# A graph layer with a routed feed-forward: compares and half of the scaling move from VectorE to GpSimd

## The chip, the cores and the metric

One core of a Trainium2 chip runs the kernel as one program. The metric is the device time of one execution in microseconds (us); the shorter the better. The engines are TensorE (PE, with its weight loads as PEld), VectorE (DVE), ScalarE (ACT), GpSimd (POOL) and SyncE (SP, here only an issuer of DMAs).

## The reference, cut to what matters

There are 6250 nodes with 256 features, 100,000 edges sorted by destination, and 4 heads of 64 features.

```python
h = layernorm(x)
messages = (h @ Wf.T)[src] * direction[:, 0:1] + (h @ Wr.T)[src] * direction[:, 1:2]
scores = leaky_relu(einsum('ef,hf->eh', messages, attn[0]), 0.2)
e = exp(scores - scores.max(axis=0))
norm = e / (segment_sum(e, dst)[dst] + 1e-10)
x = x + concat over heads of segment_sum(messages * norm[:, head], dst)
# then: a top-1 router over 8 experts with a capacity, relu feed-forward 256 -> 1024 -> 256 in the
# chosen expert, times the router's probability, added to x
```

What the change touches is the message of an edge: the row of the source node has a forward half and a reverse half, each is scaled by a number of that edge, and they are added. Then every message goes to its destination's sum.

## The kernel before, in words

**Node table.** A first stage normalises the nodes, multiplies them with both weight matrices and writes a table `node_tab` to memory, one row of 136 numbers per node: 68 forward (64 features and 4 score parts) and 68 reverse.

**Tiles and batches.** The edges lie in 782 tiles of 128, one edge per partition. `order` lists 66 batches of tiles: 64 of them have GB = 12 tiles, one has 4 and the last has 10. GT = 6 is half a batch. `srci` holds the source node of each edge, `ea` its two factors, `local` the place of its destination among the at most 128 nodes of its group.

**One batch** goes through these functions:

- `gathers(b)` (L983): for each tile one indirect DMA on GpSimd's queue (L989) that fetches 128 rows of the table into one of three `gt` buffers. In the second half of a batch it also issues waiting `put` calls (L1198): scatters of routed rows into the experts' buffer `buf`, one behind a gather.
- `messages(b)` (L995): on VectorE, copies both factors of the batch into `fixed`, which lies in PSUM (L1002), scales the forward halves in place (L1004, 128x816), then for each half batch scales the reverse halves into the PSUM tile `rv` (L1009) and adds both into `m` (L1011); then the scores (L1014 to L1022) and on ScalarE their exponentials (L1024).
- `places(b)` (L1027): one VectorE compare (L1032, 128x1536) that makes `hot`, for each tile a 128x128 matrix of zeros and ones which says to which destination each edge belongs. Its operands are the column numbers (`lane_p`, in `fixed`) and `local`.
- `products(b)` (L1035): VectorE spreads message times weight over the four heads (L1041, 128x3072).
- `windows(b, half)` (L1054): TensorE adds up the messages by destination, one matmul per tile with `hot` as weights (L1073); finished groups are copied and stored to `sums`.

**The order of work** is written out by hand (the pools run under a manual schedule). The loop over b from 0 to NB = 66 calls `messages(b)`, `windows(b - 1, 0)`, `places(b)`, `products(b)`, `windows(b - 1, 1)`, and, at its end, `gathers(b + 3)`; three batches of gathers are issued ahead of the loop. Between these calls stand pieces of two other jobs: the router for nodes whose sums are complete (`route`, which among much else runs L1121 and L1122 on VectorE and hands the `put` calls to the gathers), and, from b = 13, pieces of the experts' feed-forward (L1351 and L1369 on TensorE). How many pieces go between two calls is fixed by written-down costs when the program is built. Behind the loop come the rest of the router and the rest of the feed-forward, and the fetching of results (L1401). Each engine works through its own queue in this order.

Of the kernel before, what the change touches and what calls it, by code (L numbers as in the profile page):

```python
# [8 lines left out]
F32 = mybir.dt.float32  # L9
I32 = mybir.dt.int32  # L10
AF = mybir.ActivationFunctionType
OP = mybir.AluOpType
AX = mybir.AxisListType

P = 128
# [504 lines left out]
def kernel(  # L520
# [27 lines left out]
    nc = tc.nc  # L548
# [13 lines left out]
    MS = O + H  # L562
    ROW = 2 * MS
# [6 lines left out]
    GB = 12  # L570
# [10 lines left out]
    GT = GB // 2  # L581
# [24 lines left out]
    node_tab = dram.tile([N, ROW], F32, name="node_tab")  # L606
# [38 lines left out]
    lane = const.tile([P, P], F32, name="lane")  # L645
# [55 lines left out]
    srci = ep.tile([P, EW], I32, name="srci")  # L701
    ea = ep.tile([P, 2, EW], F32, name="ea")
    local = ep.tile([P, ET], F32, name="local")
# [45 lines left out]
    with tc.tile_pool(name="p1", bufs=2) as p1, \  # L749
# [19 lines left out]
        for c, tiles in enumerate(parts):  # L769
            k = len(tiles)  # L770
# [86 lines left out]
    def clear(r):  # L857

        nc.sync.dma_start(buf[r:r + 512, 0:D].rearrange("(p n) d -> p n d", n=4),
                          zeros.rearrange("p (n d) -> p n d", n=4))  # L860

    def clear_last(e):

        r0, r1 = e * TOT + OFF[NP - 2], (e + 1) * TOT
        J = (r1 - r0) // P
        nc.sync.dma_start(ybuf[r0:r1, :].rearrange("(p n) d -> p (n d)", n=J), zeros[:, 0:J * D])
        r0 = e * TOT + OFF[NP - 1]
        J = (r1 - r0) // P
        nc.sync.dma_start(buf[r0:r1, D:BW].rearrange("(p n) k -> p n k", n=J),
                          zeros[:, 0:J * (D + 2)].rearrange("p (n k) -> p n k", k=D + 2))  # L870
# [7 lines left out]
    order = [(i, min(i + GB, TOP)) for i in range(HEAD, TOP, GB)]  # L878
# [3 lines left out]
    NB = len(order)  # L882
# [59 lines left out]
    with tc.tile_pool(name="p4", bufs=1) as p4, tc.tile_pool(name="p5", bufs=2) as p5, \  # L942
# [3 lines left out]
        p2 = edge_pools.enter_context(tc.tile_pool(name="p2", bufs=2))  # L946
# [4 lines left out]
        lane_p, shift_p = fixed[:, 0:P], fixed[:, P:P + H]  # L951

        def turn(b, k0, k1):
            o = P + H + b % 2 * (2 + H) * GB
            return fixed[:, o + k0 * GB:o + k1 * GB]

        def spread(t):

            pm = ps2.tile([P, H, P], F32, name="pm", tag="acc", bufs=4)
            for hd in range(H):  # L960
                nc.tensor.transpose(pm[:, hd, :], t[:, hd:hd + 1].to_broadcast([P, P]), ident)
            return pm
# [16 lines left out]
            got.append(over)  # L979


        gts, vs = {}, {}
        pool_work = []  # L983

        def gathers(b):
            i0, i1 = order[b]
            gts[b] = p2.tile([P, GB, ROW], F32, name="gt", bufs=3)
            for i in range(i0, i1):
                nc.gpsimd.indirect_dma_start(  # L989
                    out=gts[b][:, i - i0, :], out_offset=None, in_=node_tab,  # L990
                    in_offset=bass.IndirectOffsetOnAxis(ap=srci[:, i:i + 1], axis=0))
                if i - i0 >= GT and pool_work:
                    pool_work.pop(0)()

        def messages(b):  # L995

            i0, i1 = order[b]
            n = i1 - i0
            gt = gts.pop(b)
            m = p2.tile([P, GB, MS], F32, name="m")  # L1000
            fac = turn(b, 0, 2).rearrange("p (k j) -> p k j", k=2)
            nc.vector.tensor_copy(fac[:, :, :n], ea[:, :, i0:i1])  # L1002
            fw = gt[:, :n, 0:MS]
            nc.vector.tensor_mul(fw, fw, fac[:, 0, :n].unsqueeze(2).to_broadcast([P, n, MS]))  # L1004
            for a0 in range(0, n, GT):
                a1 = min(a0 + GT, n)
                k = a1 - a0
                rv = ps2.tile([P, GT, MS], F32, name="rv")
                nc.vector.tensor_mul(rv[:, :k, :], gt[:, a0:a1, MS:ROW],  # L1009
                                     fac[:, 1, a0:a1].unsqueeze(2).to_broadcast([P, k, MS]))  # L1010
                nc.vector.tensor_add(m[:, a0:a1, :], fw[:, a0:a1, :], rv[:, :k, :])  # L1011
            sc = p2.tile([P, GB, H], F32, name="sc")
            s = sc[:, :n, :]
            nc.vector.scalar_tensor_tensor(s, m[:, :n, O:MS], 0.2, m[:, :n, O:MS],  # L1014
                                           op0=OP.mult, op1=OP.max)
            if i1 == ET:
                nc.vector.tensor_scalar(sc[:, n - 1, :], sc[:, n - 1, :], no_edge, None, op0=OP.add)
            nc.vector.tensor_reduce(gmax[:, b, :], s.rearrange("p j h -> p h j"), AX.X, OP.max)
            if b == 0:
                nc.vector.tensor_reduce(shift, spread(gmax[:, 0, :]), AX.X, OP.max)  # L1020
                nc.vector.tensor_copy(shift_p, shift)
            nc.vector.tensor_sub(s, s, shift_p.unsqueeze(1).to_broadcast([P, n, H]))  # L1022
            v = p2.tile([P, GB, ACC], F32, name="v")
            nc.scalar.activation(v[:, :n, H * O:ACC], s, AF.Exp)  # L1024
            vs[b] = m, v

        def places(b):  # L1027

            i0, i1 = order[b]
            n = i1 - i0  # L1030
            hot = p2.tile([P, GB, P], F32, name="hot")
            nc.vector.tensor_tensor(hot[:, :n, :], lane_p.unsqueeze(1).to_broadcast([P, n, P]),  # L1032
                                    local[:, i0:i1].unsqueeze(2).to_broadcast([P, n, P]), OP.is_equal)
            vs[b] += (hot,)

        def products(b):
            n = order[b][1] - order[b][0]
            m, v, hot = vs[b]
            w = turn(b, 2, 2 + H).rearrange("p (j h) -> p j h", h=H)
            nc.vector.tensor_copy(w[:, :n, :], v[:, :n, H * O:ACC])  # L1040
            nc.vector.tensor_mul(  # L1041
                v[:, :n, 0:H * O].rearrange("p n (h o) -> p n h o", h=H),
                m[:, :n, 0:O].unsqueeze(2).to_broadcast([P, n, H, O]),
                w[:, :n, :].unsqueeze(3).to_broadcast([P, n, H, O]))

            vl = p2.tile([P, ACC], F32, name="vl")
            nc.scalar.copy(vl, v[:, n - 1, :])  # L1047
            vs[b] = v, hot, vl

        taken = {"released": 0, "passes": 0, "before": None, "pv": None, "rows": 0, "jobs": 0, "fetched": 0}  # L1050

# [376 lines left out]
        def routes_of(c):  # L1428
            nonlocal next_p
            for cost in route(c, next_p):  # L1430
                yield cost
            if chunks[c][-1] == LASTS[next_p]:
                end_pass(next_p)
                wait_pass.append(next_p)
                next_p += 1
                if next_p < NP:
                    begin_pass(next_p)
                yield 0.0

        def step_routing():  # L1440
            nonlocal credit
            while routing:
                cost = next(routing[0], None)
                if cost is None:
                    routing.pop(0)
                    continue
                credit -= cost
                break

        def step_experts(share):  # L1450
            nonlocal credit
            credit = min(credit + share, share)
            while credit > 0 and b > 12:
                cost = step_ffn()
                if cost is None:
                    break
                credit -= cost

        for b in range(3):
            gathers(b)  # L1460
        for b in range(NB + 1):
            if 4 <= b < 4 + E:
                clear(1024 * (b - 4))
                clear(1024 * (b - 4) + 512)
                clear_last(b - 4)
            if b < NB:
                messages(b)
            step_routing()
            if b:
                windows(b - 1, 0)  # L1470
            step_experts(SHARE / 2)
            step_routing()
            if b < NB:
                places(b)
            step_routing()
            if b < NB:
                products(b)
            step_routing()
            if b:
                windows(b - 1, 1)  # L1480
            taken["released"] = taken["rows"]
            step_experts(SHARE / 2)
            while next_c < len(chunks) and done_at[next_c] < b:
                routing.append(routes_of(next_c))
                next_c += 1
            step_routing()
            pool_work.extend(todo)
            del todo[:]
            if b + 3 < NB:
                gathers(b + 3)  # L1490
            if wait_pass and not pool_work:
                taken["rows"] = wait_pass.pop() + 1
                i = (taken["rows"] - 1) * E
                if taken["jobs"] >= i - 1:
                    fetch_rows(i)
                    fetch_rows(i + 1)
# [115 lines left out]
```

## Time and profile before

| | us |
|---|---|
| median of 9 runs | 1447.16 (1445.01 to 1455.39) |
| the profiled execution, its own time | 1445.53 |
| its span, from the first to the last instruction | 1443.6 |
| first gather starts, last gather ends | 75.66, 1143.69 |
| mean granted TensorE clock | 0.851 of full speed |

Busy time by stage, from the view that cuts the span into windows:

| window, us | PE | DVE | ACT | POOL | clock |
|---|---|---|---|---|---|
| 75.6 to 300 | 108.2 | 131.0 | 13.3 | 169.8 | 0.70 |
| 300 to 569 | 145.8 | 193.5 | 29.8 | 204.1 | 0.71 |
| 569 to 1143.8 | 507.1 | 456.3 | 133.3 | 421.7 | 0.90 |
| 1143.8 to 1443.6 | 269.3 | 135.9 | 96.8 | 65.7 | 0.96 |

The profile has several views. One line gives each engine's busy time. Another cuts the span into 40 equal slices and gives the busy share of each in tenths. Groups of instructions have the line, the engine, what is written from what and how often; behind the first bar the busy time in us and the mean in ns, behind the second the idle time of the engine just ahead of them and what ended it. In the order of time, each row has its start, its duration, and in brackets the gap ahead of it. "issue" is a gap in which the engine waited for nothing that the profile shows.

### The profile page before, as it was taken

How to read it: one execution, taken by the hardware profiler on the slowest of the kernel's cores; microseconds unless marked ns; L12 is line 12 of the kernel's file. 1: busy time of each engine (PE TensorE's matmuls, PEld its weight loads, DVE VectorE, ACT ScalarE, POOL GpSimd, SP SyncE). 2: the span in 40 equal slices, each digit the busy share in tenths (PEclk: the TensorE clock that was granted, in tenths of full speed). 3: DMA queues.
4: the chain of work that ended last, by engine and by line, in shares of the span. 5: the costliest groups of instructions: out<-in, count | busy, mean ns of one | idle time of the engine just before them, and what ended most of it. 6: DMA issues, size and time to landing. Idle time of an engine off the chain costs nothing.

```text
span 1443.6 us, 15046 instructions
## 1 busy us (share of the span) xinstructions
PE 1082.9 (75%) x4658; PEld 867.0 (60%) x4658; DVE 970.5 (67%) x2062; ACT 305.7 (21%) x771; POOL 863.5 (60%) x912
## 2 busy tenths in 40 slices
PE   6815554647447461979898998887889998999895
PEld 5614443435335341767676776665668787888774
DVE  6836556587578584576969978869799734315772
ACT  3500000010011010222222222222222132233441
POOL 0067777777777777767777777775677502003424
PEclk9957677767667766989898998897889999999998
DMA  7412565462332343448475665665565445767992
GB/s 226 131 50 64 174 210 166 146 194 74 76 103 72 80 111 93 129 136 224 136 195 165 189 196 169 157 194 152 158 190 158 143 161 193 246 212 247 305 310 71
DMA packets 160583, 231.22 MB, mean 160 GB/s; under 512 B 19760, under 2 KB 130542, under 8 KB 160366
## 3 DMA queue, kind: packets, MB, share of 16 engines
q1 hardware_dynamic: 125354, 152.34, 32.8%
q0 software_dynamic: 32064, 75.13, 20.1%
q10 hardware_dynamic: 3076, 2.69, 0.6%
q8 instruction: 39, 0.64, 0.2%
q14 instruction: 50, 0.41, 0.1%
HBM read 167.19 MB, written 63.70 MB: 160 GB/s over the span
## 4 chain that ended last, share of the span: by engine, by line
PE 27%; POOL 22%; DMA 18%; DVE 18%; issue 11%; ACT 2%; SPq 0%; DVEq 0%; POOLq 0%; ACTq 0%
POOL gt L989 20%; PE py L1369 7%; PE ph L1351 7%; PE pv L1073 6%; DMA sums<-r 4%; DMA part<-sums 4%; DVE v L1041 4%; DMA gt<-node_tab,srci 3%; PE pl L1142 2%; DMA yg<-ybuf,to_get 2%; PE pn L783 2%; DVE ln_st L673 1%; DVE hot L1032 1%; POOL buf L1198 1%; DVE hx L1122 1%
## 5 line engine op out<-in xcount | busy, mean ns | idle before, releaser
L989 POOL DMA_INDIRECT gt<-node_tab,srci x782 | 748.0, 956 | 255.9 <-issue 231.7
L1073 PE MATMUL pv<-v,hot 128*128 128x260 f32 x1564 | 459.0, 446 | 139.2 <-DVE v L1041 132.6
L1073 PEld LDWEIGHTS pv<-v,hot 128*128 128x128 f32 x1564 | 337.0, 224 | 243.2 <-issue 185.6
L1351 PE MATMUL ph<-xT,w1t 128*128 128x256 f32 x1024 | 238.6, 387 | 6.9 <-DVE y L1277 6.3
L1369 PE MATMUL py<-w2t,hf 128*128 128x256 f32 x1024 | 228.4, 380 | 2.3 <-ACT hf L1354 2.2
L1041 DVE TENSOR_TENSOR v<-m,fixed 128x3072 f32<-128x3072 f32 (+1 forms) x66 | 218.7, 3313 | 2.3
L1351 PEld LDWEIGHTS ph<-xT,w1t 128*128 128x128 f32 x1024 | 198.3, 194 | 36.4 <-DVE y L1277 7.5
L1369 PEld LDWEIGHTS py<-w2t,hf 128*128 128x128 f32 x1024 | 192.4, 190 | 28.4 <-ACT hf L1354 3.4
L1004 DVE TENSOR_TENSOR gt<-gt,fixed 128x816 f32<-128x816 f32 (+1 forms) x66 | 65.6, 993 | 156.4 <-DMA gt<-node_tab,srci 151.7
L1354 ACT ACTIVATE hf<-ph,b1t 128x256 f32<-128x256 f32 x256 | 105.9, 469 | 178.4 <-PE ph L1351 178.1
L1401 POOL DMA_INDIRECT yg<-ybuf,to_get x49 | 48.8, 996 | 149.1 <-DMA xr<-x_d 79.9
L1032 DVE TENSOR_TENSOR hot<-fixed,local 128x1536 f32<-128x1536 f32 (+1 forms) x66 | 114.1, 1730 | 0.0
L1198 POOL DMA_INDIRECT buf<-hx,to_put x49 | 48.6, 991 | 70.8 <-DVE kept L1219 46.7
L1134 PE MATMUL pt<-ident,hx 128*128 128x128 f32 x98 | 22.6, 400 | 88.7 <-DVE hx L683 88.7
L1024 ACT ACTIVATE v<-sc 128x48 f32<-128x48 f32 (+1 forms) x66 | 16.0, 242 | 324.5 <-DVE sc L1022 324.5
L1277 DVE TENSOR_TENSOR y<-py,b2b 128x512 f32<-128x512 f32 x32 | 22.0, 687 | 91.3 <-PE py L1369 91.3
L1011 DVE TENSOR_TENSOR m<-gt,rv 128x408 f32<-128x408 f32 x131 | 75.5, 577 | 4.5
L1047 ACT COPY vl<-v 128x260 f32<-128x260 f32 x66 | 26.9, 407 | 242.8 <-DVE v L1041 180.2
L1009 DVE TENSOR_TENSOR rv<-gt,fixed 128x408 f32<-128x408 f32 x131 | 76.2, 581 | 2.2
L1134 PEld LDWEIGHTS pt<-ident,hx 128*128 128x128 f32 x98 | 17.0, 203 | 94.5 <-DVE hx L683 54.5
L1077 ACT COPY r<-pv 128x260 f32<-128x260 f32 x87 | 32.2, 370 | 111.7 <-PE pv L1073 111.6
L1142 PEld LDWEIGHTS pl<-gw,ht 128*128 128x128 f32 x196 | 41.8, 323 | 3.3 <-ACT ht L1136 3.2
(221 smaller groups left out, 892.1 us busy)
## 6 DMA issues: line engine op xcount, KB each, us to landing
w1t<-in_L_ffn_w_dram SPq DMA_DIRECT2D x32, 1024.0 KB
w2t<-in_L_ffn_w_dram SPq DMA_DIRECT2D x32, 1024.0 KB
gt<-node_tab,srci POOLq DMA_INDIRECT x782
sums<-r SPq DMA_DIRECT2D x85, 125.9 KB
buf<-zeros SPq DMA_DIRECT2D x16, 512.0 KB
xe<-buf SPq DMA_DIRECT2D x32, 256.0 KB
part<-sums SPq DMA_DIRECT2D x12, 520.0 KB
x_d<-hx SPq DMA_DIRECT2D x12, 512.0 KB
```

What stands on the lines that cost most here:

```text
L989: nc.gpsimd.indirect_dma_start(out=gts[b][:, i - i0, :], out_offset=None, in_=node_tab, in_offset=bass.IndirectOffsetOnAxis(ap=srci[:, i:i ...
L1004: nc.vector.tensor_mul(fw, fw, fac[:, 0, :n].unsqueeze(2).to_broadcast([P, n, MS]))
L1009: nc.vector.tensor_mul(rv[:, :k, :], gt[:, a0:a1, MS:ROW], fac[:, 1, a0:a1].unsqueeze(2).to_broadcast([P, k, MS]))
L1011: nc.vector.tensor_add(m[:, a0:a1, :], fw[:, a0:a1, :], rv[:, :k, :])
L1032: nc.vector.tensor_tensor(hot[:, :n, :], lane_p.unsqueeze(1).to_broadcast([P, n, P]), local[:, i0:i1].unsqueeze(2).to_broadcast([P, n, P]) ...
L1041: nc.vector.tensor_mul(v[:, :n, 0:H * O].rearrange("p n (h o) -> p n h o", h=H), m[:, :n, 0:O].unsqueeze(2).to_broadcast([P, n, H, O]), w[ ...
L1073: nc.tensor.matmul(pv, hot[:, i - i0, :], v[:, i - i0, :], start=(i == g0), stop=(i == g1 - 1))
L1142: nc.tensor.matmul(pl[:, n, :], hts[n // 2][:, n % 2, d, :], gw[:, d, :], start=(d == 0), stop=(d == DC - 1))
L1198: ins = nc.gpsimd.indirect_dma_start(out=buf, out_offset=bass.IndirectOffsetOnAxis(ap=to_put[:, n0 + n:n0 + n + 1], axis=0), in_=hx[:, n, ...
L1351: nc.tensor.matmul(ph[:, f - f0, :], w1t[:, d, f * P:(f + 1) * P], xT[:, d, :S], start=(d == 0), stop=(d == DC - 1))
L1354: nc.scalar.activation(hf[:, f, :S], ph[:, f - f0, :], AF.Relu, bias=b1t[:, e * FC + f:e * FC + f + 1])
L1369: nc.tensor.matmul(py[:, j - j0, :], hf[:, f, j * P:(j + 1) * P], w2t[:, f, :], start=(f == 0), stop=(f == FC - 1))
```

## The change

GpSimd takes over two steps of VectorE.

- The compare: `places(b, i)` now makes one tile of `hot` (128x128) on GpSimd, with the column numbers in SBUF (`lane`) and the tile's column of `local` as a scalar per partition. While batch b is gathered, each gather is followed by one compare for a tile of batch b - 1.
- The forward scaling: `scaled(b - 1)` multiplies the forward halves of the previous batch in place on GpSimd, behind the sixth gather of batch b and its compare, with the factors read from `ea` in SBUF.

`gt` gets four buffers instead of three, and `hot` four instead of two. `messages` copies only the reverse factors and no longer scales the forward halves. The loop calls `gathers(b + 3)` also for b + 3 = NB, which issues no gather but the last batch's compares and its scaling. An optional `put` stands between a gather and the compare.

```diff
-        gts, vs = {}, {}
+        gts, vs, places_of = {}, {}, {}
         def gathers(b):
+            i0, i1 = order[b] if b < NB else (0, 0)
+            if b < NB:
+                gts[b] = p2.tile([P, GB, ROW], F32, name="gt", bufs=4)
+            for i in range(GB):
+                if i < i1 - i0:
+                    nc.gpsimd.indirect_dma_start(
+                        out=gts[b][:, i, :], out_offset=None, in_=node_tab,
+                        in_offset=bass.IndirectOffsetOnAxis(ap=srci[:, i0 + i:i0 + i + 1], axis=0))
+                    if i >= GT and pool_work:
+                        pool_work.pop(0)()
+                if b:
+                    places(b - 1, i)
+                if b and i == GT - 1:
+                    scaled(b - 1)
+
+        def scaled(b):
+
             i0, i1 = order[b]
-            gts[b] = p2.tile([P, GB, ROW], F32, name="gt", bufs=3)
-            for i in range(i0, i1):
-                nc.gpsimd.indirect_dma_start(
-                    out=gts[b][:, i - i0, :], out_offset=None, in_=node_tab,
-                    in_offset=bass.IndirectOffsetOnAxis(ap=srci[:, i:i + 1], axis=0))
-                if i - i0 >= GT and pool_work:
-                    pool_work.pop(0)()
+            n = i1 - i0
+            fw = gts[b][:, :n, 0:MS]
+            nc.gpsimd.tensor_mul(fw, fw, ea[:, 0, i0:i1].unsqueeze(2).to_broadcast([P, n, MS]))
...
-            fac = turn(b, 0, 2).rearrange("p (k j) -> p k j", k=2)
-            nc.vector.tensor_copy(fac[:, :, :n], ea[:, :, i0:i1])
+            fac = turn(b, 0, 1)
+            nc.vector.tensor_copy(fac[:, :n], ea[:, 1, i0:i1])
             fw = gt[:, :n, 0:MS]
-            nc.vector.tensor_mul(fw, fw, fac[:, 0, :n].unsqueeze(2).to_broadcast([P, n, MS]))
...
-        def places(b):
+        def places(b, i):
             i0, i1 = order[b]
-            n = i1 - i0
-            hot = p2.tile([P, GB, P], F32, name="hot")
-            nc.vector.tensor_tensor(hot[:, :n, :], lane_p.unsqueeze(1).to_broadcast([P, n, P]),
-                                    local[:, i0:i1].unsqueeze(2).to_broadcast([P, n, P]), OP.is_equal)
-            vs[b] += (hot,)
+            if not i:
+                places_of[b] = p2.tile([P, GB, P], F32, name="hot", bufs=4)
+            if i < i1 - i0:
+                nc.gpsimd.tensor_scalar(places_of[b][:, i, :], lane, local[:, i0 + i:i0 + i + 1], None, op0=OP.is_equal)
...
-            if b < NB:
-                places(b)
...
-            if b + 3 < NB:
+            if b + 3 <= NB:
                 gathers(b + 3)
```

More of the change, by code (lines that the diff above doesn't have):

```diff
@@ L1009, in messages @@
                 nc.vector.tensor_mul(rv[:, :k, :], gt[:, a0:a1, MS:ROW],
-                                     fac[:, 1, a0:a1].unsqueeze(2).to_broadcast([P, k, MS]))
+                                     fac[:, a0:a1].unsqueeze(2).to_broadcast([P, k, MS]))
                 nc.vector.tensor_add(m[:, a0:a1, :], fw[:, a0:a1, :], rv[:, :k, :])
@@ L1025, in messages @@
             vs[b] = m, v
-        def places(b):
+        def places(b, i):
             i0, i1 = order[b]
-            n = i1 - i0
-            hot = p2.tile([P, GB, P], F32, name="hot")
-            nc.vector.tensor_tensor(hot[:, :n, :], lane_p.unsqueeze(1).to_broadcast([P, n, P]),
-                                    local[:, i0:i1].unsqueeze(2).to_broadcast([P, n, P]), OP.is_equal)
-            vs[b] += (hot,)
+            if not i:
+                places_of[b] = p2.tile([P, GB, P], F32, name="hot", bufs=4)
+            if i < i1 - i0:
+                nc.gpsimd.tensor_scalar(places_of[b][:, i, :], lane, local[:, i0 + i:i0 + i + 1], None, op0=OP.is_equal)
         def products(b):
             n = order[b][1] - order[b][0]
-            m, v, hot = vs[b]
+            m, v = vs[b]
             w = turn(b, 2, 2 + H).rearrange("p (j h) -> p j h", h=H)
@@ L1047, in products @@
             nc.scalar.copy(vl, v[:, n - 1, :])
-            vs[b] = v, hot, vl
+            vs[b] = v, places_of.pop(b), vl
         taken = {"released": 0, "passes": 0, "before": None, "pv": None, "rows": 0, "jobs": 0, "fetched": 0}
```

## The prediction

> **What bounds the kernel now.** I read the busy shares first, then the slices, then the groups, then GpSimd's rows in order of time. The summary alone misleads: it puts GpSimd (POOL) at 60%, below TensorE.
>
> ```profile
> PE 1082.9 (75%) x4658; PEld 867.0 (60%) x4658; DVE 970.5 (67%) x2062; ACT 305.7 (21%) x771; POOL 863.5 (60%) x912
> POOL 0067777777777777767777777775677502003424
> L989 POOL DMA_INDIRECT gt<-node_tab,srci x782 | 748.0, 956 | 255.9 <-issue 231.7
> ```
>
> The slices show GpSimd at a flat seven tenths from about 75 to 1144 us, and the group line shows why it is seven and not ten: 782 gathers of 0.956 us, and ahead of them 231.7 us of "issue", idle time in which the engine waited for nothing that the profile shows. In order of time (start, duration, then the gap ahead) it looks like this wherever one cuts it:
>
> ```profile
> 119.57 0.94 POOL L989 DMA_INDIRECT gt<-node_tab,srci  x1 [0.30 <-issue]
> 120.81 0.94 POOL L989 DMA_INDIRECT gt<-node_tab,srci  x1 [0.30 <-issue]
> 122.06 0.94 POOL L989 DMA_INDIRECT gt<-node_tab,srci  x1 [0.31 <-issue]
> 123.31 0.95 POOL L989 DMA_INDIRECT gt<-node_tab,srci  x1 [0.30 <-issue]
> ```
>
> Gathers start every 1.248 us (47 of them from 94.61 to 153.27), whatever else runs. Up to 1143.7 us there are 782 of them and 48 of the scatters of L1198, so 830 x 1.248 = 1036 us of the 1068 us between the first and the last of them. Real waits are few: for a free `gt` buffer 11.5 us in 4 waits (10.3 beyond the usual 0.30 each), for rows to scatter 10.9 us in 4 (9.7 beyond), so 20 us; stretched gathers make up most of the rest. VectorE (DVE) is busy 780.8 us of the same 1068 and waits 150.4 us for gathers. So GpSimd alone sets the length of the edge stage. Behind it lie 300 us (1143.8 to 1443.6) in which TensorE is busy 269; the program's order fixes what it does there, so a longer edge stage moves the end one for one. The chain that ended last gives the gathers only 20% of the span; it follows whatever ended last in each batch, and between 569 and 1090 us VectorE and TensorE keep so close behind GpSimd that it walks through them. That GpSimd hardly waits there either is what decides.
>
> **What goes from VectorE.** Per batch of 12 tiles, the compare (L1032, 1.750 us) and the forward multiply (L1004, 1.004 us); the small copy of factors halves from 24 to 12 columns. That is 112.0 + 64.3 us of busy time over the full batches. I cost it at nothing won: VectorE and TensorE already wait for gathers.
>
> **What comes to GpSimd.** 782 compares of 128x128 (one behind each gather, or at the end with no gather) and 66 multiplies (64 of 128x816, one of 272, one of 680). Neither operation is in the trace on this engine. What there is of plain arithmetic stands at the start of the program:
>
> ```profile
> 0.32 0.10 POOL L1598 MEMSET const-float32-0.0<- 128x1 f32 x1 [0.32 <-issue]
> 0.35 0.11 POOL L1598 MEMSET const-float32-1.0<- 128x1 f32 x1
> ...
> 1.21 0.28 POOL masks.py:199 TENSOR_SCALAR_AFFINE_SELECT ident<-ident 128x128 f32<-128x128 f32 x1
> 1.45 0.28 POOL L625 TENSOR_SCALAR_AFFINE_SELECT upto<-upto 128x128 f32<-128x128 f32 x1
> 1.69 0.19 POOL L629 MEMSET first_row<- 128x128 f32 x1
> 1.83 0.09 POOL L640 MEMSET no_edge<- 128x1 f32 x1
> ```
>
> Rows overlap here, so I take start to start, not durations.
>
> - *Compare.* The affine select has the same shape and one read operand: 1.21 to 1.45, 0.24 us. Above: 0.33, if the per-partition scalar costs what a 128x1 memset lasts (0.09). Below: 0.03, the smallest start to start (0.32 to 0.35), if its work lies in the 0.30 us gap ahead of the next gather. I take 0.24, the same shape: 782 x 0.24 = 188 us.
> - *Multiply.* A select of 128x128 lasts 0.283 and one of 128x1 0.177, so 0.106 us for 127 columns, 0.835 ns a column. Two operands read in turn: 816 x 1.67 ns = 1.36, and the fixed 0.18: 1.54 us. Over all 66: 53,176 columns x 1.67 ns = 89 us, and 66 x 0.18 = 12, together 101 us. Below: VectorE's own 1.004, 66 us; above: twice that, 2.0, 132 us.
> - *Nothing below zero* for either: GpSimd loses no instruction in exchange; the gathers and scatters stay in number and order.
>
> The Trainium skill, GPSIMD Engine Reference, section "Elementwise — side-by-side cycle accounting", speaks against this move: it gives a two-input operation on GpSimd about 2.6 cycles a column at 1.2 GHz and calls VectorE about twice as fast. By it the multiply would be an estimated 1.77 us before any fixed cost and the sum some 15 to 20 us more than mine; no row of this trace shows it.
>
> **Waits that are added.** (1) The multiply waits until its batch has landed. It stands behind six gathers of the next batch, at least 6 x 1.248 = 7.5 us after the last gather that it needs; queued behind it are the other six gathers. The last gathers of three batches landed 1.9, 5.1 and 3.6 us after their issue ended (VectorE's multiply at 122.40, 1136.29 and 1147.25 against 120.5, 1131.2 and 1143.7). So no stall; each microsecond of lateness in every batch would cost 66. (2) TensorE's matmul of a tile waits for that tile's compare, which comes with the next batch's gathers, about a batch later than the rows. `gt` and `hot` have four buffers in exchange, so a gather waits for a batch consumed about three batches earlier, and a compare for matmuls four batches back. With VectorE relieved of 2.75 us a batch I count the 20 us of present waits as gone. (3) At the very end six compares fall into the 3.6 us in which the last rows land; then the multiply (680 columns, 1.3 us) takes the place of VectorE's 0.86 + 1.48. Nothing either way.
>
> **Contention.** A gather is longer when VectorE reads two SBUF operands:
>
> ```profile
> 622.17 1.79 POOL L989 DMA_INDIRECT gt<-node_tab,srci  x1 [0.31 <-issue]
> ...
> 624.26 0.96 POOL L989 DMA_INDIRECT gt<-node_tab,srci  x1 [0.30 <-issue]
> ```
>
> At 621.92 and 623.17 ran L1121 and L1122, both operands in SBUF, 1.22 and 1.23 us: 0.85 us lost. Over all gathers that is 782 x (956 - 944) ns = 9 us. The added instructions add a quarter to what GpSimd does, so 2 us more; left out. The multiplies and the copy that stay on VectorE keep an operand in PSUM (`fixed`, `rv`).
>
> **The sum**, against the profiled execution (1445.53 us, span 1443.6; the median of the runs is 1447.16, so 1.6 more): 1445.5 + 188 + 101 - 20 = **1714 us**.
>
> **Rivals.**
>
> - *The compares hide in the gap.* The 0.30 us ahead of every gather belongs to nothing that the profile shows. If it is preparation of the next gather that leaves GpSimd's arithmetic free, a compare of 0.24 fits in, and only 0.03 each is left: 1445.5 + 23 + 101 - 20 = 1549 us. For it: 0.24 is less than 0.30, and arithmetic rows overlap each other at the start. Against it: gathers never overlap each other; whatever fills the gap has held the engine up 830 times, and the stretched gathers move their successor by the full delay.
> - *Each change of kind costs a gap of its own.* If gather to compare and compare to gather both bring 0.30, another 848 x 0.30 = 254 us: 1968 us. For it: a gap before every gather without exception. Against it: none between unlike arithmetic rows at the start (memset, select, iota).
> - *Faster: GpSimd's arithmetic runs beside the gathers altogether.* If a gather occupies only part of GpSimd for its 0.94 us, compares and multiply cost the gathers nothing, and what remains is the 20 us of waits won by the fourth buffer and a lighter VectorE: 1426 us. It decides when less than 20 / 66 = 0.3 us of the 4.4 us a batch is uncovered. Against it: the gathers' even beat in every load of the DMA engines says that GpSimd itself is the limit, and a multiply needs all 128 partitions of it.
> - *The change doesn't do what it says*: the order of the built program shows one compare behind each gather and the multiply behind the sixth, so this has no share.
>
> The skill's Perfetto Trace Analysis, "DMA Instruction — SWDGE (GPSIMD)", has two of GpSimd's eight cores write the descriptors while each core has a queue of its own; six could start a compare early, but those two set the pace, which speaks for the first sum. No row here shows single cores.
>
> **Chances.** 0.61 for the sum of 1714 (1609 to 1836 with its bounds: below 782 x 0.15, a 128x128 memset's start to start, and 66; above 782 x 0.33 and 132 with no waits won); 0.22 for hidden compares (1515 with VectorE's price of the multiply, to 1580); 0.11 for the extra gaps; 0.06 for no cost. The range takes in the first two, 1520 to 1830. A measurement of this kernel can tell about 0.3% from no change: faster by more 0.05, within 0.02, slower 0.93.
>
> **What would show it.** Start to start of gathers: 1.49 with a compare between (1.28 if hidden, 1.8 with two gaps), and some 3 us across the multiply (1.54 more). The last gather at about 1413 instead of 1143, the stretch behind it still near 300 us. VectorE near 46% (970.5 - 176 - 6 of 1714), waiting for GpSimd's multiply in nearly every batch. I am wrong if the gathers keep their 1.25, if the multiply waits for a DMA with an idle time over 0.3, or if the stretch behind the edge stage changes by over 20 us.

## The result and the profile after

The changed kernel takes 2006.86 us (median of 10 runs, 2005.12 to 2011.51) against 1448.71 (median of 31): 1.386 times as long, 95% interval 1.384 to 1.388. The profiled execution took 2007.9 us, its span is 2005.9. The direction was forecast, the size was not: 558 us instead of some 270, beyond the upper end of the range. Ten of the runs told below (e1 to e4 and e8 to e13) stand beside slower runs of the kernel before, 1813 to 1847 us at a mean granted TensorE clock of 0.77 in place of 0.85, of which no trace is kept, so such a run is read only where its own trace shows what set its pace.

The same lines of the page as before the change (busy us, share of the span, instructions; then GpSimd's tenths in 40 slices; then groups):

```profile
PE 1155.3 (58%) x4658; PEld 909.0 (45%) x4658; DVE 819.7 (41%) x1930; ACT 303.2 (15%) x771; POOL 1527.8 (76%) x1760
...
POOL 0388888888888888898888888888888888220343
...
POOL 64%; PE 11%; issue 10%; DMA 8%; DVE 6%; ACT 1%; SPq 0%; POOLq 0%; DVEq 0%
...
L992 POOL DMA_INDIRECT gt<-node_tab,srci x782 | 813.3, 1040 | 144.1 <-issue 131.5
L1046 POOL TENSOR_SCALAR hot<-lane,local 128x128 f32<-128x128 f32 x782 | 499.0, 638 | 26.9
L1024 DVE TENSOR_TENSOR m<-gt,rv 128x408 f32<-128x408 f32 x131 | 75.5, 577 | 859.2 <-POOL gt L1007 856.4
L1007 POOL TENSOR_TENSOR gt<-gt,ea 128x816 f32<-128x816 f32 (+1 forms) x66 | 102.3, 1551 | 0.0
```

GpSimd's busy plateau is longer and a tenth higher, and the chain that ended last now runs through GpSimd for 64% of the span where it was 22% (the line before: `PE 27%; POOL 22%; DMA 18%; DVE 18%; issue 11%; ACT 2%; SPq 0%; DVEq 0%; POOLq 0%; ACTq 0%`). The 782 compares take 499 us, 0.638 each; the prediction had 188. The 66 multiplies take 102, where it had 101. VectorE gave its work away and waits 856 us for the multiply instead. Where the time went by place is plain from the gathers: the last one starts at 1704.7, not 1142.7, and the stretch behind the edge stage is as long as it was. The view by windows, one line for the edge stage and one for the rest (the window and its length; then busy us of PE, PEld, DVE, ACT and POOL with their instructions; then the granted clock, the DMA engines' share and GB/s):

```profile
76.60:1705.80 1629.20, 832.73 (x3067) 631.25 (x3068) 633.72 (x1377) 174.31 (x434) 1451.10 (x1665) 0.71 0.33 95
1705.80:2005.90 300.10, 269.55 (x1252) 233.11 (x1252) 131.86 (x318) 96.57 (x231) 74.46 (x80) 0.96 0.63 210
```

That is 1629 us for an edge stage that was 1068, and 300.1 us behind it, where it was 299.8. GpSimd in order of time, across a multiply:

```profile
99.32 1.03 POOL L992 DMA_INDIRECT gt<-node_tab,srci  x1 [0.17 <-issue]
100.38 0.62 POOL L1046 TENSOR_SCALAR hot<-lane,local 128x128 f32<-128x128 f32 x1
101.18 1.03 POOL L992 DMA_INDIRECT gt<-node_tab,srci  x1 [0.17 <-issue]
102.24 0.63 POOL L1046 TENSOR_SCALAR hot<-lane,local 128x128 f32<-128x128 f32 x1
102.83 1.56 POOL L1007 TENSOR_TENSOR gt<-gt,ea 128x816 f32<-128x816 f32 x1
104.56 1.05 POOL L992 DMA_INDIRECT gt<-node_tab,srci  x1 [0.17 <-issue]
```

A gather follows the last after 1.864 us (ten of them from 106.44 to 125.08) where it was 1.248, so a compare adds 0.616 (0.618 in the expectations below). Across the multiply it is 3.38, so the multiply adds 1.51. 782 x 0.616 + 66 x 1.51 = 581, less the 20 us of waits: 561. The profiled executions differ by 562.4 (2007.9 - 1445.53).

The trace holds one test already. At the end of the edge stage compares run with no gather between them (rows of one kind merged, x9):

```profile
1704.71 1.03 POOL L992 DMA_INDIRECT gt<-node_tab,srci  x1 [0.17 <-issue]
1705.78 5.23 POOL L1046 TENSOR_SCALAR hot<-lane,local 128x128 f32<-128x128 f32 x9
1710.98 1.32 POOL L1007 TENSOR_TENSOR gt<-gt,ea 128x680 f32<-128x680 f32 x1
```

From 1705.78 to 1710.98 are 5.20 us for nine, 0.578 each. So a compare costs nearly all of its 0.616 by itself; only 0.04 comes from standing between gathers. That speaks for the theory which the runs were to test, *GpSimd pays each compare in full and a compare is simply dear*, against the rivals *a gap is paid at every change between gather and arithmetic* and *part of it hides in the gap ahead of a gather*. What then makes a compare dear (its scalar per partition, the comparing, its columns, or a price per instruction) was open.

### The profile page after: what moved, and what is told of

Read it like the earlier page. It is cut to its first block, busy times and chain, and to the rows that moved or that the text cites. A ratio compares the mean times of both kernels' runs of the same rounds, so it can differ in the third digit from the quotient of the medians.

```text
span 2005.9 us, 16036 instructions
## 1 busy us (share of the span) xinstructions
PE 1155.3 (58%) x4658; PEld 909.0 (45%) x4658; DVE 819.7 (41%) x1930; ACT 303.2 (15%) x771; POOL 1527.8 (76%) x1760
## 4 chain that ended last, share of the span: by engine, by line
POOL 64%; PE 11%; issue 10%; DMA 8%; DVE 6%; ACT 1%; SPq 0%; POOLq 0%; DVEq 0%
POOL gt L992 35%; POOL hot L1046 22%; POOL gt L1007 4%; PE ph L1363 3%; PE py L1381 3%; DMA out_dram<-o 2%; DMA gt<-node_tab,srci 2%; POOL buf L1210 2%; PE pv L1085 2%; PE pn L783 1%; DVE v L1053 1%; DVE o L1327 1%; DVE m L1024 1%; DMA yg<-ybuf,to_get 1%; DVE rv L1022 1%
## 5 line engine op out<-in xcount | busy, mean ns | idle before, releaser
L992 POOL DMA_INDIRECT gt<-node_tab,srci x782 | 813.3, 1040 | 144.1 <-issue 131.5
L1085 PE MATMUL pv<-v,hot 128*128 128x260 f32 x1564 | 509.1, 484 | 338.5 <-DVE v L1053 327.9
L1085 PEld LDWEIGHTS pv<-v,hot 128*128 128x128 f32 x1564 | 370.3, 246 | 460.7 <-issue 316.7
L1046 POOL TENSOR_SCALAR hot<-lane,local 128x128 f32<-128x128 f32 x782 | 499.0, 638 | 26.9
L1381 PE MATMUL py<-w2t,hf 128*128 128x256 f32 x1024 | 237.0, 388 | 47.5 <-ACT hf L1366 36.2
L1007 POOL TENSOR_TENSOR gt<-gt,ea 128x816 f32<-128x816 f32 (+1 forms) x66 | 102.3, 1551 | 0.0
L1022 DVE TENSOR_TENSOR rv<-gt,fixed 128x408 f32<-128x408 f32 x131 | 76.6, 585 | 21.0 <-issue 13.2
L961 PE MATMUL pm<-ident,top_s 128*128 128x128 f32 x56 | 13.4, 386 | 101.9 <-DVE top_s L968 57.1
L961 PEld LDWEIGHTS pm<-ident,top_s 128*128 128x128 f32 x56 | 8.9, 193 | 106.9 <-DVE top_s L968 58.6
```

The costliest lines, as they stand in the source:

```text
L992: nc.gpsimd.indirect_dma_start(out=gts[b][:, i, :], out_offset=None, in_=node_tab, in_offset=bass.IndirectOffsetOnAxis(ap=srci[:, i0 + i:i ...
L1007: nc.gpsimd.tensor_mul(fw, fw, ea[:, 0, i0:i1].unsqueeze(2).to_broadcast([P, n, MS]))
L1022: nc.vector.tensor_mul(rv[:, :k, :], gt[:, a0:a1, MS:ROW], fac[:, a0:a1].unsqueeze(2).to_broadcast([P, k, MS]))
L1046: nc.gpsimd.tensor_scalar(places_of[b][:, i, :], lane, local[:, i0 + i:i0 + i + 1], None, op0=OP.is_equal)
L1085: nc.tensor.matmul(pv, hot[:, i - i0, :], v[:, i - i0, :], start=(i == g0), stop=(i == g1 - 1))
L1381: nc.tensor.matmul(py[:, j - j0, :], hf[:, f, j * P:(j + 1) * P], w2t[:, f, :], start=(f == 0), stop=(f == FC - 1))
```

## The experiments

**One part of the change at a time.** e1 keeps the compares on GpSimd and puts the multiply back on VectorE; e2 the other way round. Both keep the four `gt` buffers. The main lines of the edits:

```diff
 # e1, against the changed kernel
-                if b and i == GT - 1:
-                    scaled(b - 1)
...
+            nc.vector.tensor_mul(fw, fw, fac[:, 0, :n].unsqueeze(2).to_broadcast([P, n, MS]))
 # e2, against the changed kernel
-                if b:
-                    places(b - 1, i)
...
+            if b < NB:
+                places(b)          # VectorE, as before the change
```

> Compares on GpSimd, forward multiply back on VectorE. Theory (each compare costs GpSimd about 0.62 us by itself, nothing hidden, and the end follows GpSimd one for one): 1446 - 20 + 782 x 0.618 = 1909 us, a gather every 1.87 us without exception. Rival (a gap is paid at every change between gather and arithmetic, and the multiply shares one with its compare): the same here, so 1909 too, but then the multiply alone is dearer than 1.52 us. Rival (compare and multiply slow each other down): clearly below 1909.

Measured: 1904.87 us, gathers 1.86 apart:

```profile
499.94 1.03 POOL L992 DMA_INDIRECT gt<-node_tab,srci  x1 [0.17 <-issue]
501.00 0.63 POOL L1045 TENSOR_SCALAR hot<-lane,local 128x128 f32<-128x128 f32 x1
501.81 1.03 POOL L992 DMA_INDIRECT gt<-node_tab,srci  x1 [0.17 <-issue]
```

GpSimd sets the edge stage here (75.6 to 1602.3 us): behind the first gather no gather and no scatter in it waits over 0.3 us. So the run can be read: the compares alone are worth some 456 us over 1448.71, where 782 x 0.616 - 20 is 462, and compare and multiply do not slow each other down.

> Multiply on GpSimd, compares back on VectorE. Theory: 66 x 1.52 = 100 us, less the 20 us of waits that four buffers end: 1526 us; gathers on both sides of a multiply 1.248 + 1.5 us apart, all others 1.248. Rival (a gap for every change of kind): another 66 x 0.3 = 20 us, 1546. Rival (part of it hides beside gathers): below 1500.

That run (1862.35 us) and two repeats of it (e9, median 1919.57, and e11, 1882.71) tell nothing of the forecast, because GpSimd does not set the edge stage there: in e2 it waits 126.9 us in five waits for line L1014 of VectorE before scatters, and TensorE stands 231.9 us before its L1084 with no cause that the profile shows. The same kernel ran once more as e14, beside a run of before of 1449.79 us:

> Multiply alone on GpSimd, one look by itself. Theory: 1446 + 66 x 1.48 - 20 = 1523 us, the last gather at about 1224. Rival (part hides): below 1500. A run of before near 1830 beside it would make it tell nothing of either.

Measured: 1539.05 us, 89 more than that run of before. GpSimd in e14, in order of time across a multiply:

```profile
129.27 0.95 POOL L992 DMA_INDIRECT gt<-node_tab,srci  x1 [0.30 <-issue]
130.53 0.94 POOL L992 DMA_INDIRECT gt<-node_tab,srci  x1 [0.30 <-issue]
131.49 1.56 POOL L1005 TENSOR_TENSOR gt<-gt,ea 128x816 f32<-128x816 f32 x1
133.21 0.99 POOL L992 DMA_INDIRECT gt<-node_tab,srci  x1 [0.16 <-issue]
134.50 0.94 POOL L992 DMA_INDIRECT gt<-node_tab,srci  x1 [0.30 <-issue]
```

2.68 us from gather to gather, and 1.29 to the next: 1.47 more than two plain beats. The gap ahead of the gather shrinks from 0.30 to 0.16, but the gather is longer by 0.05 and the multiply lasts 1.56: of those, under 0.1 us is saved. Nothing else hides. 66 x 1.47 = 97, less 89 measured, leaves 8 us of the 20 that were counted as won. The trace agrees: GpSimd's waits before scatters are still there (7.8, 2.1 and 1.7 us), those before gathers nearly gone (the longest lasts 1.6). It does not come out to the microsecond: against the profile before, the last gather starts 86 us later (1228.9, 1142.7), and the stretch behind it is 7 longer, which no term explains. In the changed kernel, with a slower GpSimd, all 20 are gone: behind the first gather, no gather and no scatter of the edge stage waits over 0.3 us.

**Does something short hide in the gap?** e8 is the kernel before with a compare of one column behind each gather.

```diff
+        extra = p4.tile([P, ET], F32, name="extra")
...
+                nc.gpsimd.tensor_scalar(extra[:, i:i + 1], lane[:, 0:1], local[:, i:i + 1], None, op0=OP.is_equal)
```

> The kernel before with a compare of one column behind each gather, into a tile that nothing reads; all else as before. If the fixed part of a compare (0.245 us, from halves of 0.412 and wholes of 0.578 back to back) is paid in full: 1446 + 782 x 0.25 = 1640 us, a gather every 1.50 us. If what is shorter than the 0.30 us gap ahead of a gather hides in it: a gather every 1.25 to 1.28 us and 1446 to 1470 us.

Measured: 1672.14 us. GpSimd sets the edge stage here too (behind the first gather no wait in it is over 0.3 us). In order of time:

```profile
503.02 1.03 POOL L990 DMA_INDIRECT gt<-node_tab,srci  x1 [0.16 <-issue]
504.09 0.31 POOL L995 TENSOR_SCALAR extra<-lane,local 128x1 f32<-128x1 f32 x1
504.56 1.03 POOL L990 DMA_INDIRECT gt<-node_tab,srci  x1 [0.16 <-issue]
```

It is 1.54 us from gather to gather: even one column, whose row is as short as the gap, adds 0.29. (782 x 0.29 = 227, less the 20 us of waits that are gone here as well, is 207; the last gather starts 216 us later than before, and the stretch behind it is 11 longer, which no term explains.) The gap does get shorter, but the gather itself longer (1.03 for 0.94), and 0.03 comes between: 1.03 + 0.03 + 0.16 = 1.22 of the 1.248. So at most 0.03 us of the gap is room, and this rival has fallen.

**What makes a compare dear.** e4 cuts every compare in two halves:

```diff
-                nc.gpsimd.tensor_scalar(places_of[b][:, i, :], lane, local[:, i0 + i:i0 + i + 1], None, op0=OP.is_equal)
+                for c in range(0, P, P // 2):
+                    nc.gpsimd.tensor_scalar(places_of[b][:, i, c:c + P // 2], lane[:, c:c + P // 2], local[:, i0 + i:i0 + i + 1], None, op0=OP.is_equal)
```

> The changed kernel with each compare cut into two of 64 columns each. If a compare's 0.58 to 0.62 us is mostly a price per instruction, a half costs nearly the same and the time rises by 782 x 0.4 to 0.55: 2320 to 2440 us. If it is a price per column (0.18 us fixed, as for a 128x1 select, and 3.1 ns a column), a half takes 0.38 us and the time rises by 782 x 0.18 = 141: about 2150. If the fixed part is as small as the 0.03 us between two small memsets: about 2030.

Measured: 2214.0 us, 207 more than the changed kernel, between the second and the first case and nearer to the second. GpSimd sets the edge stage here too, with no wait over 0.3 us behind the first gather. At the end of its edge stage 18 halves run back to back:

```profile
1905.69 7.43 POOL L1047 TENSOR_SCALAR hot<-lane,local 128x64 f32<-128x64 f32 x18
1913.10 1.32 POOL L1007 TENSOR_TENSOR gt<-gt,ea 128x680 f32<-128x680 f32 x1
```

7.41 / 18 = 0.412 a half, against 0.578 a whole: 64 columns cost 0.166 us, 2.6 ns each, and the fixed part is 0.245. Of a whole compare 0.333 is columns. The one column of e8 agrees: (0.616 - 0.29) / 127 = 2.6 ns.

The next three change what is computed. In each the kernel then takes its general path as well, behind the first, and the total time (5107.53 to 5439.56 us) holds both. So the forecasts of the total do not apply; the edge stage, which comes first, is read from the trace. e5 takes a constant for the scalar per partition:

```diff
-                nc.gpsimd.tensor_scalar(places_of[b][:, i, :], lane, local[:, i0 + i:i0 + i + 1], None, op0=OP.is_equal)
+                nc.gpsimd.tensor_scalar(places_of[b][:, i, :], lane, 5.0, None, op0=OP.is_equal)
```

> The changed kernel with the compares against the constant 5.0 in place of the scalar per partition; the sums by destination are left wrong. If the scalar per partition makes the compare dear, a compare falls to the 0.24 to 0.28 us of a select of the same shape, and the time to about 2007 - 782 x 0.35 = 1730 us. If the operation or the columns do, it stays near 2007.

Measured:

```profile
1730.04 5.38 POOL L1046 TENSOR_SCALAR hot<-lane 128x128 f32<-128x128 f32 x9
1735.50 1.33 POOL L1007 TENSOR_TENSOR gt<-gt,ea 128x680 f32<-128x680 f32 x1
```

Nine in a row take 5.46 us to the start of the multiply, 0.607 each, and gathers are 1.90 apart. The scalar per partition is not the price. e6 multiplies in place of comparing (`op0=OP.mult`):

> The changed kernel with a multiply in place of the compare, same operands (column numbers times the scalar per partition); the sums by destination are left wrong. If comparing is slow on GpSimd, an instruction falls to 0.3 to 0.4 us and the time to 1760 to 1830 us. If the scalar per partition or the columns make it dear, it stays near 2007.

Measured:

```profile
1685.42 5.24 POOL L1046 TENSOR_SCALAR hot<-lane,local 128x128 f32<-128x128 f32 x9
1690.63 1.32 POOL L1007 TENSOR_TENSOR gt<-gt,ea 128x680 f32<-128x680 f32 x1
```

Nine take 5.21 us, 0.579 each, as for the compare; gathers are 1.84 apart. Comparing is not the price either. e7 does away with the 12 single instructions:

```diff
-            if i < i1 - i0:
-                nc.gpsimd.tensor_scalar(places_of[b][:, i, :], lane, local[:, i0 + i:i0 + i + 1], None, op0=OP.is_equal)
+            if i == GT - 1:
+                n = i1 - i0
+                nc.gpsimd.tensor_tensor(places_of[b][:, :n, :], lane.unsqueeze(1).to_broadcast([P, n, P]),
+                                        local[:, i0:i1].unsqueeze(2).to_broadcast([P, n, P]), OP.subtract)
```

> The changed kernel with, in place of a batch's 12 compares, one two-operand subtract of 128x1536 ahead of the multiply (column numbers minus places); it leaves the compare out, so the sums by destination are wrong. If two-operand arithmetic costs 0.21 us and 1.67 ns a column, as the multiply shows (1.568 us for 816 columns, 0.661 for 272), it takes 2.77 us, a batch costs GpSimd 15.0 + 1.5 + 2.8 us plus its scatters, and the time is 1446 - 20 + 100 + 66 x 2.77 = 1709 us. If a batch's compare work is dear in any form: 1900 or more.

Its rows in order of time:

```profile
505.67 0.94 POOL L992 DMA_INDIRECT gt<-node_tab,srci  x1 [0.30 <-issue]
506.63 2.77 POOL L1047 TENSOR_TENSOR hot<-lane,local 128x1536 f32<-128x1536 f32 x1
509.34 1.56 POOL L1007 TENSOR_TENSOR gt<-gt,ea 128x816 f32<-128x816 f32 x1
511.06 0.97 POOL L992 DMA_INDIRECT gt<-node_tab,srci  x1 [0.16 <-issue]
```

2.77 us, as worked out from the multiply's rows; the edge stage is 1318 us (76.6 to 1394.5) where the theory had 1068 - 20 + 100 + 66 x 2.77 = 1331. So two-operand arithmetic on GpSimd (this subtract and the multiply) is 1.67 ns a column, and the one-operand form with a scalar, which the change uses, 2.6: the form with *fewer* operands is the dearer one. Why it is dearer no run shows.

Is it the place? The prediction's price came from selects at the quiet start of the program. The general path in e5 runs two such selects back to back 2 ms later, just behind indirect DMAs:

```profile
2022.57 0.98 POOL L1554 DMA_INDIRECT out_dram<-xm,row_l  x1 [0.31 <-DVE zeros L95]
...
2023.85 0.31 POOL masks.py:199 TENSOR_SCALAR_AFFINE_SELECT ident<-ident 128x128 f32<-128x128 f32 x1
2024.10 0.29 POOL L84 TENSOR_SCALAR_AFFINE_SELECT before<-before 128x128 f32<-128x128 f32 x1
2024.34 0.21 POOL L87 MEMSET upto<- 128x128 f32 x1
```

0.25 and 0.24 us from start to start, as at the beginning. So the start of the program is not what made the select cheap. A select between the gathers of the edge stage was not run.

**Four buffers.** What is left of the sum is the 20 us of waits. e3 is the kernel before with one change:

```diff
-            gts[b] = p2.tile([P, GB, ROW], F32, name="gt", bufs=3)
+            gts[b] = p2.tile([P, GB, ROW], F32, name="gt", bufs=4)
```

> The kernel before with four gt buffers instead of three and nothing else. Theory (the four waits of a gather for a free gt, 10 us beyond the usual gap, are all that buffers can give): 7 to 10 us less than before, ratio 0.993 to 0.995. Rival (those waits only move to the scatters, which wait for VectorE's rows): within 0.3% of before.

> The kernel before with four gt buffers once more, beside runs of the kernel before near 1447 us. Theory (the waits of gathers for a free gt are all that buffers can give): 7 to 10 us less, ratio 0.993 to 0.995. Rival (those waits move to the scatters, which wait for VectorE's rows): within 0.3%.

In three of four (e3, e10, e12) it was slower than the runs of before beside it (medians of 1823 to 1835 us): ratio 1.066 (1.061 to 1.071), 1.069 (1.063 to 1.074), 1.068 (1.062 to 1.074). The fourth, e13, is a single run of 1979.57 beside one of 1832.02. TensorE in e13, matmuls in order of time, over a stretch in the middle:

```profile
643.32 0.59 PE L1073 MATMUL pv<-v,hot 128*128 128x260 f32 x1 [2.20 <-issue]
646.12 0.59 PE L1073 MATMUL pv<-v,hot 128*128 128x260 f32 x1 [2.22 <-issue]
648.91 0.59 PE L1073 MATMUL pv<-v,hot 128*128 128x260 f32 x1 [2.20 <-issue]
```

There is one matmul in 2.8 us, with a gap that no wait explains; GpSimd waits 176.4 us in this run for a free `gt`. So the forecast of 7 to 10 us gained is neither borne out nor refuted: in none of the four is GpSimd the limit. Why TensorE runs so there, and whether the fourth buffer has a part in it, is open; e14 and the changed kernel have four buffers as well, and no such stretch of TensorE sets their pace.

## Why the prediction was wrong, point by point

- **What bounds the kernel** was right: the flat beat of gathers, and the end that follows it one for one (edge stage +561 us, behind it +0.3). VectorE's relief was costed at nothing; VectorE now waits 856 us for GpSimd. Its busy time was forecast at 788 us (46%) and is 819.7: some of its instructions got longer (L683 on `hx` takes 0.50 us on average, 0.41 before).
- **The compare** is the step that failed: "I take 0.24, the same shape: 782 x 0.24 = 188 us." It measured 0.616, 482 us. The row it came from, an affine select of 128x128, has the shape and the operand count of the compare, but another price: its columns cost 0.835 ns, the compare's 2.6 (e4, e8). The compare's fixed part, 0.245, is alone as much as a whole select from start to start. With 0.616 the sum is 1445.5 + 482 + 101 - 20 = 2008.5, against 2007.9. The form of the sum held; this term was too small by 294 us.
- **The upper bound** failed with it: 0.33 was the select plus a price for the scalar, and the scalar costs nothing (e5). No row showed this form on GpSimd; a wider bound was at hand in the slope that the prediction itself gave the multiply (0.18 + 128 x 1.67 ns = 0.39), and even that falls short of 0.58.
- **The multiply** was right in size: 1.54 worked out, 1.57 lasted, 1.51 added, and (1.568 - 0.661) / 544 columns = 1.67 ns, twice the select's 0.835. The reason given, "two operands read in turn", is not shown by this, and the same slope for one operand missed the compare by a factor of three; part of the hit may be luck.
- **The waits** were right in the changed kernel: the multiply never waits for its rows, and the buffer waits went.
- **Hidden compares** (0.22): fell by e8. The argument held that a compare shorter than the gap could fit in it; of the 0.30 us at most 0.03 was room.
- **A gap for each change of kind** (0.11): its 1968 us is near the result by chance. A compare between gathers costs 0.04 more than one that follows another compare, not 0.30; the nine compares with no gather between them are nearly as dear.
- **Faster, beside the gathers** (0.06): fell with e1 and e14; each part costs its full duration to within 0.1 us.

The Trainium skill, GPSIMD Engine Reference, section "Elementwise — side-by-side cycle accounting", has the two-input operation at about 2.6 cycles a column, an estimated 2.17 ns at its 1.2 GHz. Here it is 1.67. For the multiplies the prediction makes 15 to 20 us more of the page's figure; its 53,176 columns at 2.17 ns are an estimated 115 us, 14 more than its 101 without a fixed part and 26 more with 0.18 us each. The same page's "Engine selection" calls one-input operations on GpSimd roughly line-rate. This case shows 2.6 ns a column for the one-operand form, more than for two operands; the measurement decides.

## What to carry to other kernels

Where one engine's beat sets a stage, every instruction added to it is paid in full, gaps or not, until a run shows one that is not: put the smallest such instruction behind each step and look at the beat before moving work there. A duration is carried from an operation to another of the same shape only if the form is the same; where an operation has not been seen on an engine, its upper bound must be a multiple of the nearest row, not that row plus a little. Here the compare cost 2.6 times the select. And multiply the uncertainty by the count: 0.376 us too little was 294 us here, because there are 782 of them.

## What the hardware showed that was not expected

- On GpSimd a one-operand instruction with a scalar costs 0.245 us and 2.6 ns a column (e4), for both operations that were run (0.579 us for a multiply of 128 columns, 0.578 for a compare) and with a constant no less (0.607); two-operand arithmetic 0.21 us and 1.67 ns (0.661 for 272 columns, 1.568 for 816, 2.77 for 1536).
- A gather behind a compare starts after a gap of 0.16 to 0.17 us instead of 0.30, but lasts 1.03 instead of 0.94 (the changed kernel, e8).
- VectorE can be held up by GpSimd's multiply. The 49 instructions of L683 on `hx` last 0.41 us in the kernel before (shortest, median and longest in ns below); in e14 five of them overlap a multiply, and each ends 0.16 to 0.17 us after that multiply does, the longest lasting 2.3 us. VectorE's instructions with an operand in PSUM keep their time beside a multiply (0.587 us for `rv`, seven times). The prediction's contention looked only at VectorE slowing GpSimd. It costs nothing here, because VectorE is not the limit. First the kernel before, then e14:

```profile
L683 DVE TENSOR_SCALAR hx<-hx,ln_mv,ln_rs x49: 403/406/415, 318.7 to 1178.5; 128x256 f32<-128x256 f32 x49
L683 DVE TENSOR_SCALAR hx<-hx,ln_mv,ln_rs x49: 400/407/2321, 345.4 to 1266.1; 128x256 f32<-128x256 f32 x49
```

- The kernel before with one more buffer was 7% slower than the kernel before (e3, e10, e12). In all four of its traces TensorE runs one matmul in 2.8 us for stretches (253 to 293 us of unexplained gaps before L1073, where the kernel before has 6.6); why is open.
